# Routed experts visited two pairs at a time, and the shared expert's later row loads issued by GpSimd

## The chip, the cores and the metric

The kernel runs on one core of a Trainium2 chip. The metric is the device time of one execution in microseconds. A run's time is the median of several executions; the profile comes from one more execution that the hardware profiler recorded.

## The reference

All data is float32. A sequence of 64 steps with 128 rows of 512 values goes through a GRU, then a feed-forward layer with ternary weights, a causal convolution, and at last a mixture of experts. Only the last part is touched by the change. Cut to it:

```python
# x: [8192, 512]; 64 experts, 6 of them for each token, at most 64 tokens for an expert
scores = softmax(x @ gate_w.T)
topk_w, topk_i = top_k(scores, 6)
buf = zeros((64, 64 + 1, 512)).at[flat_i, slot].set(x[token_ids])
g = einsum('ech,ehi->eci', buf, w_gate)          # [64, 65, 352]
u = einsum('ech,ehi->eci', buf, w_up)
y = einsum('eci,eih->ech', silu(g) * u, w_down)
out_slots = y[flat_i, slot] * (flat_w * valid)[:, None]
routed = out_slots.reshape(T, 6, 512).sum(axis=1)
shared = silu(x @ sw_gate) * (x @ sw_up) @ sw_down   # [8192, 704] inside
result = x_in + routed + shared
```

So each of the 64 experts has 64 slots of gathered rows, a gate, an up and a down product; the shared expert sees every row.

## The kernel before, in words

The program runs in stages: the GRU with its input products and the ternary layer (to about 1400 us), the convolution (to about 1560 us), then the shared expert in 16 blocks of 4 time steps (512 rows). The router's work is laid between the products of blocks 0 to 8. From block 9 on (about 2022 us) the routed experts are laid there instead. Only blocks 9 to 15 matter here.

**The shared expert.** `shared(i)` computes block i with a fast scheme of seven half-size products (`winograd`, L695): each product is two matmuls (four records on TensorE) into one of four PSUM tiles `y`, `psx`, `psw`, `psz`. VectorE and ScalarE empty these tiles with sums (L726, L729, L731, L738, L741) and Silu. A block begins with four wide matmuls (L869) and ends with a down product (L806, L823) whose results are written over the block's rows `xr`. Each `yield` of `shared` is a slot, 44 a block; after each one the loop at the end of the kernel may call a piece of the routed experts. After a block `add_shared` (L971) issues four adding DMAs from GpSimd, from the block's rows into the output in DRAM. Then `load_xrows(i + 2)` (L1156) issues a load of 1 MB by SP into the same buffer, from the DRAM copy `xts`. There are two such buffers.

**The routed experts.** Two experts make a pair q: one expert's 64 slots use columns 0 to 63 of TensorE, the other's columns 64 to 127, so that the matmuls of both run side by side (records with 128\*64). These are the halved columns. For a pair there are four pieces of code:

- `inputs` (L1364 to L1371): VectorE copies the router's weights of the pair out of the gathered rows into `rw`; TensorE turns the rows (L1369) into `py`, and VectorE copies them to `xeT`.
- `gate_up` (L1382 to L1391): it first issues the gather of pair q + 2 (L1340, GpSimd, three `rows` buffers). 32 matmul calls give `pg` and `pu`; ScalarE's Silu and a product on VectorE with `rw` and `pu` make `a`.
- `turn` (L1397 to L1400): it first issues the loads of the gate and up weights of pair q + 2 by SP, into the buffers that pair q's matmuls have left; then TensorE turns `a` into `py`, and VectorE copies it to `aeT`.
- `down` (L1408 to L1419): the down product into `py`; the loads of the down weights of pair q + 2; ScalarE copies `py` to `ys` (L1417, two buffers); GpSimd scatters the two halves of `ys` into the output with two indirect, adding DMAs (L1419). Each of these waits until the one before it has landed, because both add into the same DRAM tensor.

The PSUM tiles `pg`, `pu`, `py` have one buffer each; the pool `ex` (`rw`, `xeT`, `a`, `aeT`, `ys`) has two. The weights of four experts, that is of two pairs, have room at a time.

**The order.** `experts()` yields 97 pieces: inputs, gate and up of pair 0, and then for each pair `turn`, the next pair's `inputs`, and one visit of the halved columns, that is `down` of pair q with `gate_up` of pair q + 1. The loop at the end of the kernel spreads them over 23/28 of the slots of blocks 9 to 15:

```python
while due < EPIECES and due * PIECES * SPREAD < slot * 4 * EPIECES:
    next(routed)
    due += 1
```

The text above gives the order in which the program is written. A scheduler then places the instructions on their engines, and each engine runs its own in the order in which they then stand. This moves gathers ahead by some pairs, for example. What is said of an order on an engine is read from the built program or the trace. For block 15 the output so far is loaded into a row buffer as `sums`, and the block's results are added there and stored by SP.

Of the kernel before, what the change touches and what calls it, by code (L numbers as in the profile page):

```python
# [42 lines left out]
def adaln_ffn_kernel(  # L43
# [22 lines left out]
    nc = tc.nc  # L66
# [32 lines left out]
    def load_rows(dst, src):  # L99

        return nc.sync.dma_start(out=dst, in_=src.rearrange("(k p) n -> p k n", p=P))
# [568 lines left out]
    NI = T // NB  # L670
# [303 lines left out]
    with (  # L974
# [10 lines left out]
        def turn(t):  # L985

            if t in (2, 3):
                ps = ps_y.tile([P, D], F32, name="y")
            else:
                ps = ps_t1.tile([P, D], F32, name="pst1")  # L990
            ps = ps.rearrange("p (k b) -> p k b", k=KD)
            for k in range(KD):
                last = nc.tensor.transpose(ps[:, k, :], hid(t)[:, k * P : (k + 1) * P], ident)
            return ps, last

        def route(its, turned={}):


            for i in its:
                for t in range(i * NB, i * NB + NB):  # L1000
                    ps = turned[t] if t in turned else turn(t)[0]
                    with behind(marks, t in turned):
                        copied = nc.vector.tensor_copy(
                            hid(t).rearrange("p (k b) -> p k b", k=KD), ps
                        )
                    if t == NB - 1:
                        marks.append(copied)
                    if t >= TH:
                        nc.sync.dma_start(out=xts[t - TH], in_=hid(t))
                    yield  # L1010
# [104 lines left out]
        for t in (NB, NB + 1):  # L1115
            second[t], last = turn(t)
# [36 lines left out]
    def load_xrows(i):  # L1153
        if i < NI:
            xrows[i] = xrp[i % 2].tile([P, NB, D], F32, name="xr")
            nc.sync.dma_start(  # L1156
                out=xrows[i], in_=xts[i * NB - TH : (i + 1) * NB - TH].rearrange("t p d -> p t d")
            )

    row_buffer("left")  # L1160
    load_xrows(NI // 2)
    esp = ctx.enter_context(tc.tile_pool(name="es", bufs=1, reuse_waits="tile"))
    wexs = []
# [15 lines left out]
    def load_gate_up(q):  # L1179

        if q < NE // 2:
            for e in (2 * q, 2 * q + 1):
                wg = wexs[e % 4].tile([P, KD, EI], F32, name="wg")
                load_rows(wg, w_gate[e])
                wu = wexs[e % 4].tile([P, KD, EI], F32, name="wu")
                load_rows(wu, w_up[e])
                weights[e] = [wg, wu]

    def load_down(q):
        if q < NE // 2:  # L1190
            for e in (2 * q, 2 * q + 1):
                wd = wexs[e % 4].tile([P, len(ech), D], F32, name="wd")
                load_rows(wd[:, :efull, :], w_down[e, : efull * P, :])
                nc.sync.dma_start(out=wd[:n_last, efull, :], in_=w_down[e, efull * P :, :])
                weights[e].append(wd)

    weights = {}
    for q in range(2):
        load_gate_up(q)
        load_down(q)  # L1200
    load_xrows(NI // 2 + 1)

    NPAIR = NE // 2
# [125 lines left out]

    add_shared(NI // 2)
    load_xrows(NI // 2 + 2)
    gat = ctx.enter_context(tc.tile_pool(name="gat", bufs=3, reuse_waits="tile"))
    ex = ctx.enter_context(tc.tile_pool(name="ex", bufs=2, reuse_waits="tile"))
    ps_e = ctx.enter_context(tc.tile_pool(name="ps_e", bufs=1, space=PSUM))

    def gather(q):
        rows = gat.tile([P, TW], F32, name="rows")
        nc.gpsimd.indirect_dma_start(  # L1340
            out=rows,
            out_offset=None,
            in_=tab,
            in_offset=bass.IndirectOffsetOnAxis(ap=idxp[:, q : q + 1], axis=0),
        )
        return rows
# [4 lines left out]
    class Pair:  # L1351
# [5 lines left out]
        def inputs(self):  # L1357
            q = self.q
            rows = gathered.pop(q)
            self.ws = [weights.pop(2 * q + j) for j in range(2)]  # L1360

            self.rw = ex.tile([P, 1], F32, name="rw")
            for j in range(2):
                nc.vector.tensor_copy(  # L1364
                    self.rw[halves[j]], rows[halves[j], D + 2 * q + j : D + 2 * q + j + 1]
                )
            ps = ps_e.tile([P, D], F32, name="py").rearrange("p (k b) -> p k b", k=KD)
            for k in range(KD):
                nc.tensor.transpose(ps[:, k, :], rows[:, k * P : (k + 1) * P], ident)  # L1369
            self.xeT = ex.tile([P, KD, P], F32, name="xeT")  # L1370
            nc.vector.tensor_copy(self.xeT, ps)  # L1371

        def gate_up(self):
            q = self.q
            if q + 2 < NPAIR:
                gathered[q + 2] = gather(q + 2)
            pg = ps_e.tile([P, EI], F32, name="pg")
            pu = ps_e.tile([P, EI], F32, name="pu")
            for which, acc in ((0, pg), (1, pu)):
                for k in range(KD):  # L1380
                    for j in range(2):
                        nc.tensor.matmul(  # L1382
                            acc[halves[j]],
                            self.xeT[:, k, halves[j]],
                            self.ws[j][which][:, k, :],
                            start=(k == 0),
                            stop=(k == KD - 1),
                        )
            self.a = a = ex.tile([P, EI], F32, name="a")
            nc.scalar.activation(a, pg, AF.Silu)  # L1390
            nc.vector.scalar_tensor_tensor(a, a, self.rw, pu, ALU.mult, ALU.mult)  # L1391

        def turn(self):
            load_gate_up(self.q + 2)
            ps = ps_e.tile([P, D], F32, name="py").rearrange("p (k b) -> p k b", k=KD)
            for c, (i0, n) in enumerate(ech):
                nc.tensor.transpose(ps[:n, c, :], self.a[:, i0 : i0 + n], ident)  # L1397
            self.aeT = aeT = ex.tile([P, len(ech), P], F32, name="aeT")
            nc.vector.tensor_copy(aeT[:, :efull, :], ps[:, :efull, :])
            nc.vector.tensor_copy(aeT[:n_last, efull, :], ps[:n_last, efull, :])  # L1400

        def down(self):

            q = self.q
            py = ps_e.tile([P, D], F32, name="py")
            for c, (i0, n) in enumerate(ech):
                for j in range(2):
                    nc.tensor.matmul(  # L1408
                        py[halves[j]],
                        self.aeT[:n, c, halves[j]],  # L1410
                        self.ws[j][2][:n, c, :],
                        start=(c == 0),
                        stop=(c == len(ech) - 1),
                    )
            load_down(q + 2)
            ys = ex.tile([P, D], F32, name="ys")
            nc.scalar.copy(ys, py)  # L1417
            for j in range(2):
                nc.gpsimd.indirect_dma_start(  # L1419
                    out=out,  # L1420
                    out_offset=bass.IndirectOffsetOnAxis(
                        ap=(idxp[:CAP] if j == 0 else idxo)[:, q : q + 1], axis=0
                    ),
                    in_=ys[halves[j]],
                    in_offset=None,
                    compute_op=ALU.add,
                )

    EPIECES = 3 * NPAIR + 1

    def experts():
        pairs = [Pair(q) for q in range(NPAIR)]
        pairs[0].inputs()
        yield
        pairs[0].gate_up()
        yield
        for q, pair in enumerate(pairs):
            pair.turn()  # L1440
            yield
            if q + 1 < NPAIR:
                pairs[q + 1].inputs()
                yield
            pair.down()
            if q + 1 < NPAIR:
                pairs[q + 1].gate_up()
            yield

    routed = experts()  # L1450
    SPREAD = 23
    slot = due = 0
    for i in range(NI // 2 + 1, NI):
# [8 lines left out]
        for _ in shared(i, sums):  # L1462
            slot += 1
            while due < EPIECES and due * PIECES * SPREAD < slot * 4 * EPIECES:
                next(routed)
# [53 lines left out]
```

## Time and profile before

| what | value |
|---|---|
| median of 3 runs | 2658.8 us (2657.62 to 2659.84) |
| the profiled execution | 2660.39 us, span 2658.7 us |
| TensorE (PE) busy | 2633.1 us, 11959 matmul records |
| VectorE (DVE), ScalarE (ACT), GpSimd (POOL) busy | 1411.4, 422.7, 457.4 us |
| mean granted TensorE clock | 0.999 |
| DMA from 2050 to 2550 us | share of the 16 engines 0.82 to 1.07 by stretches of 50 us, 242 to 344 GB/s |
| gate and up matmuls (L1382) | 1024 records, 459 ns median |
| down matmuls (L1408) | 384 records, 592 ns median |
| first and last record of the down matmuls | 2040.9 and 2579.5 us |
| gathers (L1340) | 32, 1046 ns issue, 6.1 us to landing |
| scatters (L1419) | 64, 1422 ns issue, 7.2 and 6.4 us to landing (first and second half) |
| row loads (L1156) by SP | 8 of 1 MB, 5.7 us to landing |

How to read it: a profile shows one execution. Times are in microseconds from the span's start unless they are marked ns. PE is TensorE's matmuls, PEld its weight loads, which overlap with them. Matmuls are pipelined, so a matmul's length is more than what it costs; the distance between two starts is the cost. A line number is that of the kernel before. `out<-in` names the tiles written and read, and the form after it gives rows\*columns of the array and partitions x elements. "to landing" counts from a DMA's issue to the end of its transfer.

### The profile page before, as it was taken

How to read it: one execution, taken by the hardware profiler on the slowest of the kernel's cores; microseconds unless marked ns; L12 is line 12 of the kernel's file. 1: busy time of each engine (PE TensorE's matmuls, PEld its weight loads, DVE VectorE, ACT ScalarE, POOL GpSimd, SP SyncE). 2: the span in 40 equal slices, each digit the busy share in tenths (PEclk: the TensorE clock that was granted, in tenths of full speed). 3: DMA queues.
4: the chain of work that ended last, by engine and by line, in shares of the span. 5: the costliest groups of instructions: out<-in, count | busy, mean ns of one | idle time of the engine just before them, and what ended most of it. 6: DMA issues, size and time to landing. Idle time of an engine off the chain costs nothing. (4 is left out here: it accounts for less than half of the span.)

```text
span 2658.7 us, 31099 instructions
## 1 busy us (share of the span) xinstructions
PE 2633.1 (99%) x11959; PEld 1817.7 (68%) x11959; DVE 1411.4 (53%) x3116; ACT 422.7 (16%) x779; POOL 457.4 (17%) x519
## 2 busy tenths in 40 slices
PE   8999999999999999999999999999999999999999
PEld 5666666666666666666668767788876666666667
DVE  6555555555555555555557755666564333434344
ACT  1111111111111111111110222222321111111111
POOL 2112111111112121111114100000001222222210
PEclk9999999999999999999999999999999999999999
DMA  5323232332322222322238921122356899998952
GB/s 194 69 56 62 54 67 56 63 61 54 60 47 52 44 52 44 76 44 52 44 63 285 331 43 27 38 64 64 79 153 172 290 309 287 294 327 269 295 176 48
DMA packets 475540, 323.33 MB, mean 122 GB/s; under 512 B 328960, under 2 KB 395136, under 8 KB 473216
## 3 DMA queue, kind: packets, MB, share of 16 engines
q1 hardware_dynamic: 446800, 248.18, 33.4%
q0 software_dynamic: 28592, 73.16, 11.4%
q8 instruction: 95, 1.56, 0.2%
q14 instruction: 53, 0.43, 0.0%
HBM read 235.01 MB, written 92.55 MB: 123 GB/s over the span
## 5 line engine op out<-in xcount | busy, mean ns | idle before, releaser
L502 PE MATMUL psgh<-whh,hT 128*128 128x512 f32 x1536 | 676.3, 596 | 0.7 <-ACT hT L399 0.7
L502 PEld LDWEIGHTS psgh<-whh,hT 128*128 128x128 f32 x1536 | 287.2, 190 | 351.3 <-issue 337.2
L338 PE MATMUL psx<-wih,xp 128*128 128x256 f32 x768 | 198.5, 381 | 6.4 <-DMA wih<-in_w_ih_dram 5.9
L220 POOL DMA_DIRECT2D xn<-in_x_dram x61 | 33.8, 555 | 840.8 <-DVE x L428 829.2
L338 PEld LDWEIGHTS psx<-wih,xp 128*128 128x128 f32 x768 | 143.7, 191 | 25.7 <-issue 5.9
L512 DVE TENSOR_TENSOR n<-psgh,bhn 128x512 f32<-128x512 f32 x64 | 44.2, 691 | 175.4 <-PE psgh L502 175.4
L1391 DVE SCALAR_TENSOR_TENSOR a<-a,rw,pu 128x352 f32<-128x352 f32 x32 | 18.6, 580 | 220.9 <-PE pu L1382 220.9
L399 ACT COPY hT<-psf 128x512 f32<-128x512 f32 x64 | 37.5, 585 | 584.0 <-PE psf L393 584.0
L509 DVE TENSOR_TENSOR r<-psgh,gi 128x512 f32<-128x512 f32 x64 | 44.2, 691 | 141.6 <-PE psgh L502 141.6
L971 POOL DMA_DIRECT2D out_dram<-hid x32 | 27.6, 1000 | 454.6 <-issue 335.9
L413 POOL TENSOR_TENSOR xn<-xn,fb 128x512 f32<-128x512 f32 x64 | 80.7, 1263 | 144.6 <-DMA xn<-in_x_dram 144.6
L338 PE MATMUL psz<-wih,xs 128*128 128x256 f32 x384 | 98.7, 379 | 1.8 <-DVE gi L361 1.8
L338 PE MATMUL psy<-t,xs 128*128 128x256 f32 x384 | 99.9, 383 | 0.2 <-DVE t L289 0.2
L338 PE MATMUL psw<-t,xp 128*128 128x256 f32 x384 | 98.8, 380 | 0.4 <-DVE u L359 0.4
L338 PE MATMUL psw<-wih,xp 128*128 128x256 f32 x384 | 98.7, 379 | 0.0
L338 PE MATMUL psz<-t,xs 128*128 128x256 f32 x384 | 98.7, 379 | 0.0
L417 PE MATMUL psf<-sgn,hhi 128*128 128x512 f32 x256 | 95.0, 493 | 0.3 <-DVE hlo L407 0.3
L1408 PE MATMUL py<-wd,aeT 128*64 128x512 f32 (+1 forms) x384 | 89.5, 601 | 0.0
L353 DVE TENSOR_TENSOR p<-psx,bi 128x512 f32<-128x512 f32 x96 | 66.3, 691 | 37.5 <-PE psx L338 37.2
L515 ACT ACTIVATE n<-n 128x512 f32<-128x512 f32 x64 | 40.3, 629 | 274.1 <-DVE n L514 274.1
L695 PE MATMUL psx<-xr,swg 128*128 128x256 f32 x320 | 83.3, 383 | 0.0
L695 PE MATMUL psx<-hid,swg 128*128 128x256 f32 x320 | 82.4, 380 | 0.0
(311 smaller groups left out, 4709.9 us busy)
## 6 DMA issues: line engine op xcount, KB each, us to landing
wg<-in_w_gate_dram SPq DMA_DIRECT2D x64, 704.0 KB, 10.4
wu<-in_w_up_dram SPq DMA_DIRECT2D x64, 704.0 KB, 11.3
wd<-in_w_down_dram SPq DMA_DIRECT2D x64, 512.0 KB, 7.9
x1c<-x SPq DMA_DIRECT2D x62, 256.0 KB, 5.2
out_dram<-x SPq DMA_DIRECT2D x62, 256.0 KB, 5.5
xn<-in_x_dram POOLq DMA_DIRECT2D x61, 256.0 KB, 4.1
xp<-in_xT_dram POOLq DMA_DIRECT2D x30, 512.0 KB, 5.3
xc<-x1c SPq DMA_DIRECT2D x28, 512.0 KB, 8.2
```

The costliest lines, as they stand in the source:

```text
L220: (nc.sync if t < 3 else nc.gpsimd).dma_start(out=xn, in_=x[:, t, :])
L338: i = nc.tensor.matmul(ps, self.ops[n][:, k, :], self.ws[n][:, k, :], start=(first and k == 0), stop=(k == HK - 1), skip_group_check=not f ...
L353: add(self.p1, both, b)
L399: nc.scalar.copy(hT, ps)
L413: nc.gpsimd.tensor_add(xn, xn, fb)
L417: nc.tensor.matmul(ps, piece[:, k, :], sgn[:, k, :], start=(i == 0 and k == 0), stop=(i == 1 and k == KD - 1),)
L502: nc.tensor.matmul(ps, hT[:, k, :], whh[c][:, k, :], start=(k == 0), stop=(k == KD - 1))
L509: nc.vector.tensor_add(r, ps_r, gis.pop((t, 0)))
L512: nc.vector.tensor_add(n, ps_n, bhn)
L515: nc.scalar.activation(n, n, AF.Tanh)
L695: i = nc.tensor.matmul(ps.rearrange("p (j b) -> p j b", b=P) if len(r.shape) == 3 else ps, lhs(k), r, start=(first and k == 0), stop=(k == ...
L1408: nc.tensor.matmul(py[halves[j]], self.aeT[:n, c, halves[j]], self.ws[j][2][:n, c, :], start=(c == 0), stop=(c == len(ech) - 1),)
```

## The change

Four things are changed.

1. The row loads of blocks 10 to 15 are issued by GpSimd and no longer by SP. Those of blocks 8 and 9 stay on SP.
2. `experts()` takes two pairs in a round: `turn` of both, `inputs` of the next two, and then one visit with `down` q, `gate_up` q + 2, `down` q + 1, `gate_up` q + 3. At the start the inputs of pairs 0 and 1 come first, and then both their `gate_up`.
3. The loads of the gate and up weights of pair q + 2 are issued in `gate_up`, behind the matmuls, and no longer in `turn`.
4. The pieces are 81 and no longer 97, which changes their spacing in slots. The weights are kept in a dictionary by expert and kind, since gate, up and down weights are now stored in another order.

```diff
     def load_xrows(i):
         if i < NI:
             xrows[i] = xrp[i % 2].tile([P, NB, D], F32, name="xr")
-            nc.sync.dma_start(
+
+            (nc.sync if i < NI // 2 + 2 else nc.gpsimd).dma_start(
                 out=xrows[i], in_=xts[i * NB - TH : (i + 1) * NB - TH].rearrange("t p d -> p t d")
             )
...
-                weights[e] = [wg, wu]
+                weights.setdefault(e, {}).update({0: wg, 1: wu})
...
-                weights[e].append(wd)
+                weights.setdefault(e, {})[2] = wd
...
-            self.ws = [weights.pop(2 * q + j) for j in range(2)]
+            self.ws = [weights[2 * q + j] for j in range(2)]
...
+            load_gate_up(q + 2)
             self.a = a = ex.tile([P, EI], F32, name="a")
...
         def turn(self):
-            load_gate_up(self.q + 2)
...
-    EPIECES = 3 * NPAIR + 1
+    EPIECES = 5 * NPAIR // 2 + 1

     def experts():
         pairs = [Pair(q) for q in range(NPAIR)]
-        pairs[0].inputs()
+        for pair in pairs[:2]:
+            pair.inputs()
+            yield
+        for pair in pairs[:2]:
+            pair.gate_up()
         yield
-        pairs[0].gate_up()
-        yield
-        for q, pair in enumerate(pairs):
-            pair.turn()
-            yield
-            if q + 1 < NPAIR:
-                pairs[q + 1].inputs()
+        for q in range(0, NPAIR, 2):
+            for pair in pairs[q : q + 2]:
+                pair.turn()
                 yield
-            pair.down()
-            if q + 1 < NPAIR:
-                pairs[q + 1].gate_up()
+            for pair in pairs[q + 2 : q + 4]:
+                pair.inputs()
+                yield
+            for pair in pairs[q : q + 2]:
+                pair.down()
+                if pair.q + 2 < NPAIR:
+                    pairs[pair.q + 2].gate_up()
             yield
```

## The prediction

> **What bounds the kernel now.** I read the busy times first, then the time by stretches, then TensorE's timeline in the stage that the change touches, then GpSimd's.
>
> ```profile
> PE 2633.1 (99%) x11959; PEld 1817.7 (68%) x11959; DVE 1411.4 (53%) x3116; ACT 422.7 (16%) x779; POOL 457.4 (17%) x519
> ```
>
> TensorE is busy 99% of the span. In the table by stretches (columns: span of the stretch; busy time of PE, PEld, DVE, ACT, POOL; clock; DMA share; GB/s) the routed experts, 2028 to 2580 us, look like this:
>
> ```profile
> 2150.00:2200.00 50.00, 50.00 (x276) 31.20 (x272) 18.40 (x47) 7.49 (x17) 13.03 (x10) 1.00 1.07 344
> 2200.00:2250.00 50.00, 50.00 (x257) 34.04 (x256) 20.34 (x51) 6.52 (x15) 13.22 (x12) 1.00 0.93 266
> ```
>
> No stretch from 2050 to 2600 us shows idle TensorE, the clock is full, and VectorE works 40% of the time. So a saving counts only if it shortens TensorE's own work there, and any new wait of TensorE is paid in full. But the DMA engines are as good as always busy too.
>
> One visit of the halved columns (64 of 128 columns: L1408, L1382), start and length in us:
>
> ```profile
> 2054.41 1.03 PE L695 MATMUL psz<-es,swu 128*128 128x256 f32 x4
> 2055.27 1.03 PE L695 MATMUL psx<-xr,swg 128*128 128x256 f32 x4
> 2056.23 2.80 PE L1408 MATMUL py<-wd,aeT 128*64 128x512 f32 x12
> 2058.86 2.54 PE L1382 MATMUL pg<-wg,xeT 128*64 128x352 f32 x16
> 2061.23 2.54 PE L1382 MATMUL pu<-wu,xeT 128*64 128x352 f32 x16
> 2063.69 1.13 PE L695 MATMUL psw<-xr,st 128*128 128x256 f32 x4
> 2064.66 1.03 PE L695 MATMUL psz<-es,st 128*128 128x256 f32 x4
> ```
>
> Read starts, not lengths. A product of the shared expert takes 0.86 from start to start (2054.41 to 2055.27), but 0.96 when a visit follows (2055.27 to 2056.23) and 0.97 when one came before (2063.69 to 2064.66). pg takes 2.37, and pu, with the way back behind it, 2.46. The first matmuls of a visit are longer too, as the spread of the down product (min/median/max ns) shows:
>
> ```profile
> L1408 PE MATMUL py<-wd,aeT x384: 590/592/643, 2040.9 to 2579.5; 128*64 128x512 f32 x128, 96*64 96x512 f32 x64
> ```
>
> So entering and leaving costs 0.10 + 0.05 + 0.09 + 0.11 = **0.35 us** a visit, beside 2.63 + 2.37 + 2.37 = 7.37 of work. From down to gate, both halved, nothing is added.
>
> GpSimd's queue (start, length, idle time before):
>
> ```profile
> 2125.91 3.63 POOL L971 DMA_DIRECT2D out_dram<-xr  x4 [5.49 <-issue]
> 2129.84 1.07 POOL L1340 DMA_INDIRECT rows<-tab,idxp  x1 [0.30 <-PE psx L695]
> 2136.67 1.47 POOL L1419 DMA_INDIRECT out_dram<-ys,idxp  x1 [5.75 <-ACT a L1390]
> 2144.72 1.41 POOL L1419 DMA_INDIRECT out_dram<-ys,idxo  x1 [6.58 <-DMA out_dram<-ys,idxp]
> ...
> 2196.65 1.42 POOL L1419 DMA_INDIRECT out_dram<-ys,idxp  x1 [4.33 <-DMA out_dram<-ys,idxo]
> ```
>
> GpSimd is busy 17%, yet its queue is nearly full: each scatter waits until the one before it has landed, since both add into the output. From 2136.67 to 2196.65 stand 8 scatters: 7.50 each, 15.0 for a pair, where a pair of experts comes every 15.34 (2040.9, 2056.23, 2071.6). By the DMA table's medians (7.2 and 6.4 to landing, 0.27 to the next issue) a scatter takes 7.07. This queue is the second bound.
>
> **The change, part by part.**
>
> *Visits.* Before: pair 0's gate, 31 visits of down and gate, a last down: 33. As built, the changed order has one double gate, 15 double visits, and the last two downs apart, since a shared product stands between them: 18. 15 fewer x 0.35 = **-5.2 us**, all of it on the path. Matmuls, transposes and evictions stay as many.
>
> *Within a double visit* (down q, gate q+2, down q+1, gate q+3, 14.7 us) the single PSUM buffers are met again. py comes back 4.74 after down q ends; its copy takes 0.585. pg comes back 5.0 after it ends, its Silu takes 0.463. pu comes back 5.0 later, its product takes 0.58. Covered, so 0; without the cover one such eviction, 0.6 x 16.
>
> *Weights.* The loads of gate and up move from the next pair's transposes to right behind the matmuls that free the buffer; SP issues as many. They come in bursts of two pairs. The slowest up load lands 15.6 after its issue now; the second pair's burst stands 7.4 after the first's instead of 15.3, so at most 8 more queue ahead of it: 23.6. It is issued at 14.7 of a visit and needed at 30.3 + 12.4 = 42.7, so 28 are there. 0; if the cover goes, each us late is paid once a visit, up to 16.
>
> *Row loads on GpSimd.* Six loads leave SP. GpSimd's order at a block's end becomes four adds (L971), the load, which must wait until the adds have landed because it overwrites their rows, and then the gathers. No 1 MB load from GpSimd is in the trace: its issue lies between 0.72 (512 KB, L214) and, twice that, 1.44; 256 KB takes 0.555, so 0.16 for each further 256 KB gives 1.05, which I take. SP is relieved: at 2136.02 it issued such a load just after the adds had landed, and the down weights behind it went at 2136.47, though their matmuls had ended at 2133.1. Nobody waited for them, so that gains 0.
>
> The Trainium skill, in "DMA: Bandwidth & Descriptors", section "Issuing engines are not separate DMA queues", says that the issuing engine makes no difference to a transfer, as all share 16 DMA engines, and only the sequencer's issue time is saved, usually little. By that rule this part would be worth 0 and the sum -5.2, 2653.6. The rows above say that an in-order queue costs more than its issue times, through what waits in it.
>
> *The new wait.* As built, VectorE's order after a double visit is: a, rw, a, rw, then the shared expert's sums. rw (L1364) needs the gathered rows of a pair used a whole visit later, and if they are late, the sums behind it are late, and TensorE's PSUM buffers with them. Times from a visit's first down, V: its first scatter goes at 2.63 + 0.24 + 0.585 + 0.27 = 3.7. The gather behind the block's end lands after four scatters, the adds (10.6 until the last has landed, from 2125.91), the load (1.05 + 0.3) and its own median 6.1: V + 3.7 + 4s + 12 + 6.1. With s = 7.07 that is V + 50.1, with 7.50 V + 51.8. rw wants it at the next visit's end, 14.7 + 0.2 + 0.58 = 15.5 after its start. Double visits stand 2 x 15.34 - 0.35 = 30.33 apart, more where a block ends, by the products that the built order puts between them: 42.1 after pair 2 (57.6, spare), 36.6 after pair 8 (52.1, just enough), 32.0 after pair 14 (two products fewer, -1.73, and the four wide matmuls of L869, +3.4): 47.5, **2.6 to 4.3 late**. In the fourth and fifth block the gathers stand ahead of the load. Behind that visit TensorE has 4 products and a transpose, 3.8, that need no VectorE; VectorE needs 0.3 for rw and 2 x 0.42 for two sums first. So of the lateness 2.0 are covered: +0.6 to +2.3. I take **+1.7**, nearer the dense row.
>
> *What is carried on.* The scatters of pair 16 then start 12.6 late, and in dense stretches 30.33 - 4 x 7.5 = 0.3 a visit is won back. ys has two buffers: the copy of pair 19 waits until the last scatter of pair 17 has landed, at V16 + 46.3 instead of 40.5. ScalarE's next Silu and VectorE's a come 2.0 late, which the cover above just holds. Bounds: 0, and 3 if it happens there and once more after the next block; I take **+1.0**.
>
> *Cadence.* EPIECES falls from 97 to 81 and pieces come every 3.12 products instead of 2.61: as many pairs per product. 0.
>
> Sum: -5.2 + 1.7 + 1.0 = -2.5. The profiled execution took 2660.4 (span 2658.7 and 1.7 around it), 1.6 above the runs' median of 2658.8; the profile would come to 2657.9, the median to **2656.3 us**.
>
> **Rivals.**
> 1. *Nothing waits.* The rows land in time because scatters take 7.07 or less: 2653.6. For it: VectorE works only 40%, and scatters after 2560 take 4. Against: the 7.50 of the dense stretch.
> 2. *Slower: the scatters set the pace.* In place: GpSimd's queue from 2060 to 2570. 62 scatters and 5 block ends (10.6 + 1.35 + two gathers of 1.3, 14.5) need 62s + 73; there are 510, and some 12 that the two ys buffers let it lag: it decides from s = 7.24 on. At 7.07 it needs 511, at 7.50 538: 16 too much, less the 5.2: +11, though the lighter stretches (6.6 at 2044 and 2112) halve that: 2664 to 2669. For it: gathers that used to hide in scatters' waits now stand behind the load. Against: the queue caught up several times before (ys done just ahead of the scatter at 2304.84).
> 3. *Weights late* by the bursts: each visit 1 us, 2670. Against: the 4.4 to spare.
>
> **How the numbers follow.** About 0.2% (5.3 us) is what a measurement of this kernel can tell from no change. Forecast 0.53, all within it. Rival 1 0.20: at 5.2 it lies on the border, 0.12 beyond and 0.08 within. Rival 2 0.22, all slower. Rival 3 0.05: 0.03 slower, 0.02 within. So faster 0.12, within 0.63, slower 0.25. The range goes from rival 1 less a run's scatter of 0.8 to the near end of rival 2 and a little more: 2652.8 to 2665.
>
> **What the changed profile would show.** The entry and exit of 0.35 only 18 times; no idle between halved products. Idle TensorE of some 2 us about 2350, put down to VectorE sums (L726, L729), with rw before them waiting for DMA rows. The lag from ys to its first scatter near 12 for pair 16. The forecast is wrong if scatters average over 7.3 there (rival 2), or if no matmul of the shared expert waits (rival 1).

## The result and the profile after

The changed kernel takes 2664.63 us (median of 11; 2662.7 to 2668.47) and the kernel before, on the same chip, 2658.18 (11; 2657.51 to 2660.34): ratio 1.0021, 95% interval 1.0013 to 1.0028. It is slower by 6.45 us; the forecast was 2.5 faster. The profiled execution took 2664.47, span 2662.8.

I read the busy times and the stretches first, as before (columns as there).

```profile
PE 2630.0 (99%) x11959; PEld 1821.9 (68%) x11959; DVE 1410.8 (53%) x3116; ACT 422.9 (16%) x779; POOL 461.9 (17%) x525
```

```profile
2150.00:2200.00 50.00, 50.00 (x271) 33.79 (x271) 20.41 (x51) 7.12 (x17) 12.52 (x10) 1.00 0.95 302
2200.00:2250.00 50.00, 50.00 (x270) 30.69 (x267) 15.96 (x40) 6.54 (x15) 12.14 (x11) 1.00 0.99 291
...
2350.00:2400.00 50.00, 40.90 (x207) 28.18 (x206) 17.46 (x48) 5.62 (x13) 14.78 (x12) 0.90 0.96 309
```

TensorE has less work than before (2630.0 against 2633.1). Every stretch of 50 us from 2050 to 2600 is full but one, and that one also has a clock of 0.90. TensorE's timeline there (start, length, and in brackets the idle time before and who ended it):

```profile
2351.53 1.03 PE L695 MATMUL psz<-es,swu 128*128 128x256 f32 x4
2352.40 0.49 PE L1398 MATMUL py<-ident,a 128*128 128x128 f32 x3
2352.72 1.03 PE L695 MATMUL psx<-xr,swg 128*128 128x256 f32 x4
2362.85 2.08 PE L695 MATMUL psw<-xr,st 128*128 128x256 f32 x4 [9.10 <-DVE u L729]
2364.72 1.91 PE L695 MATMUL psz<-es,st 128*128 128x256 f32 x4
```

One gap of 9.10 us, ended by a VectorE sum. The four matmuls after it take 1.87 from start to start, where those at 2351.53 took 0.87: half the clock. Stretches cut to the gap show it in the clock column (the last but two):

```profile
2353.00:2362.80 9.80, 0.75 (x4) 0.33 (x2) 1.14 (x5) 0.00 (x0) 3.50 (x3) 0.73 1.06 369
2362.80:2367.80 5.00, 4.95 (x12) 3.96 (x13) 2.46 (x7) 0.80 (x2) 1.41 (x1) 0.50 1.06 329
2367.80:2380.00 12.20, 12.20 (x65) 8.94 (x65) 5.63 (x13) 1.63 (x5) 4.02 (x4) 1.00 0.73 215
```

Ten records start 0.427 apart and not 0.216, and the first is 0.37 late: 2.5 us more. VectorE's timeline says why the sum was late:

```profile
2349.92 0.58 DVE L1393 SCALAR_TENSOR_TENSOR a<-a,rw,pu 128x352 f32<-128x352 f32 x1 [6.39 <-PE pu L1383]
2361.51 0.31 DVE L1365 COPY rw<-rows 64x1 f32<-64x1 f32 x2 [11.01 <-DMA rows<-tab,idxp]
2361.85 0.42 DVE L726 TENSOR_TENSOR u<-u,y 128x256 f32<-128x256 f32 x1
2362.37 0.42 DVE L729 TENSOR_TENSOR u<-psw,u 128x256 f32<-128x256 f32 x1
```

Two copies of one column each, `rw`, which nobody needs before the next visit, wait 11.01 us for a gather, and both sums stand behind them. GpSimd's queue shows what the gather stood behind:

```profile
2306.68 1.46 POOL L1420 DMA_INDIRECT out_dram<-ys,idxp  x1 [6.44 <-ACT ys L1418]
2314.26 1.42 POOL L1420 DMA_INDIRECT out_dram<-ys,idxo  x1 [6.12 <-DMA out_dram<-ys,idxp]
2322.68 1.40 POOL L1420 DMA_INDIRECT out_dram<-ys,idxp  x1 [7.00 <-ACT u L724]
2330.39 1.40 POOL L1420 DMA_INDIRECT out_dram<-ys,idxo  x1 [6.30 <-DMA out_dram<-ys,idxp]
2337.21 3.63 POOL L971 DMA_DIRECT2D out_dram<-xr  x4 [5.43 <-DMA out_dram<-ys,idxo]
2351.33 0.79 POOL L1157 DMA_DIRECT2D xr<-xts  x1 [10.48 <-DMA out_dram<-xr]
2353.00 1.05 POOL L1341 DMA_INDIRECT rows<-tab,idxp  x1 [0.89 <-PE py L1398]
```

Four scatters, four additions, the load of rows, which waits 10.48 for the additions, and only then the gather. The chain of waits gives its landing:

```profile
2353.00 8.41 DMA rows<-tab,idxp
```

To set kernels side by side I use a **stretch**: from the first product of L869 in block 9 to the last product of L823. Before it is 2022.34 to 2653.80, 631.46; after 2020.05 to 2658.00, 637.95, 6.5 more. The sum closes: 15 entries and exits saved, -5.1 (measured alone in the third experiment group below), the gap +9.1, the half clock +2.5. What lies ahead of block 9 varies by some us (its start lies between 2016.3 and 2023.8 in the eleven traces), so that medians say less than the stretch. The stretch is read from one execution, but the three kernels with one pair in a visit agree in it to 0.01.

### The profile page after: what moved, and what is told of

Its sections match the earlier page's. It is cut to its first block, busy times and chain, and to the rows that moved or that the text cites. A ratio compares the mean times of both kernels' runs of the same rounds, so it can differ in the third digit from the quotient of the medians.

```text
span 2662.8 us, 31119 instructions
## 1 busy us (share of the span) xinstructions
PE 2630.0 (99%) x11959; PEld 1821.9 (68%) x11959; DVE 1410.8 (53%) x3116; ACT 422.9 (16%) x779; POOL 461.9 (17%) x525
```

## The experiments

Medians are of 11 executions (e6: 6).

| kernel | median | before, measured alongside | ratio and 95% interval | stretch |
|---|---|---|---|---|
| the changed kernel | 2664.63 | 2658.18 | 1.0021 (1.0013 to 1.0028) | 637.95 |
| e1 pairs, loads on SP | 2659.05 | 2659.14 | 1.0001 (0.9992 to 1.0010) | 629.29 |
| e2 before, loads on GpSimd | 2658.55 | 2659.14 | 1.0000 (0.9991 to 1.0009) | 631.45 |
| e3 rw behind xeT | 2658.15 | 2659.14 | 0.9998 (0.9989 to 1.0007) | 632.70 |
| e4 load behind a gather | 2661.30 | 2659.14 | 1.0010 (1.0001 to 1.0019) | 631.84 |
| e6 e3 and four ys buffers | 2651.88 | 2659.83 | 0.9970 (0.9958 to 0.9982) | 626.36 |
| e7 e1, load behind weights | 2656.03 | 2659.83 | 0.9987 (0.9978 to 0.9996) | 629.00 |
| e8 four ys buffers only | 2665.02 | 2659.83 | 1.0018 (1.0009 to 1.0027) | 638.01 |
| e9 before, e6's two mends | 2656.82 | 2658.66 | 0.9989 (0.9980 to 0.9998) | 631.45 |
| e10 e6, loads on SP | 2656.97 | 2658.66 | 0.9993 (0.9984 to 1.0002) | 632.70 |

### First group: which part makes the gap

Theory 1 is the reading above: pairs, load and rw together make the gap. Theory 2: the load on GpSimd costs by itself. Theory 3: the pairing costs by itself, through the scatters and gathers that it brings close together.

**e1** undoes the move of the loads.

```diff
-            (nc.sync if i < NI // 2 + 2 else nc.gpsimd).dma_start(
+            nc.sync.dma_start(
```

> Two pairs in one visit, all loads of rows back on SyncE's queue. Theory 1 (the order of the two queues: VectorE's rw copy stands a visit ahead, and the gather it needs stands on GpSimd behind the load of rows, which waits until the additions have landed): without the load the gather of about 2353.0 is issued right behind the additions, about 2342, and lands at 8.4 us after that, about 2350, when VectorE comes to rw (2350.5). No wait, no clock drop, only the 15 saved entries and exits: 2653 (2652 to 2655), no gap over 1 us at L695 about 2352. Theory 2 (the load on GpSimd costs by itself, wherever rw stands): 2653 too. Theory 3 (the pairing itself costs: four scatters in a row and two gathers hold GpSimd's queue): 2663 to 2665, with the gap still there.

**e2** makes that move alone, in the kernel before.

```diff
-            nc.sync.dma_start(
+            (nc.sync if i < NI // 2 + 2 else nc.gpsimd).dma_start(
```

> The kernel before, with nothing but the later loads of rows moved to GpSimd's queue; one pair in a visit. Theory 1: here the gather issued behind the additions (2323.2 in the trace of before, put off to about 2334 by the load's wait) is wanted by rw two visits later, about 2363, so nothing is late: 2658 to 2660. Theory 2: the load's wait of about 10 us for the additions is paid here as well: 2664 to 2670. Theory 3: 2658.

**e3** moves only the two small copies on VectorE.

```diff
-            self.rw = ex.tile([P, 1], F32, name="rw")
-            for j in range(2):
-                nc.vector.tensor_copy(
-                    self.rw[halves[j]], rows[halves[j], D + 2 * q + j : D + 2 * q + j + 1]
-                )
...
-            nc.vector.tensor_copy(self.xeT, ps)
+            turned = nc.vector.tensor_copy(self.xeT, ps)
+            self.rw = ex.tile([P, 1], F32, name="rw")
+            with tc.issue_after(turned.ins):
+                for j in range(2):
+                    nc.vector.tensor_copy(
+                        self.rw[halves[j]], rows[halves[j], D + 2 * q + j : D + 2 * q + j + 1]
+                    )
```

> The changed kernel with the loads of rows left on GpSimd; only the two small copies of rw are put behind the copy of xeT on VectorE (same operations, same GpSimd order), so that the sums of the shared expert no longer stand behind them. Theory 1: the gather still lands at about 2361 but VectorE has no business with it until the transposes of the next visit, so the 9.1 us gap and the 4.6 us of half clock both go: 2653 (2652 to 2655). Theory 2 (the load holds up something other than rw, scatters or the transposes): 2659 to 2665. Theory 3: 2663 to 2665.

**e4** lets one gather go ahead of the load.

```diff
         def gather(q):
...
+        with tc.issue_after(got.ins):
+            while owed and q % 2:
+                load_xrows(owed.pop())
...
-            load_xrows(i + 2)
+            owed.append(i + 2)
```

> The changed kernel with the load of rows still on GpSimd but issued behind the next gather instead of ahead of it; the next-but-one gather stands behind it. rw is left ahead, as in the changed kernel. Theory 1: the gather goes out right behind the additions, about 2342, and lands about 2350, at most 0.5 late, which the 1.9 us that TensorE has in hand cover: 2653 (2652 to 2655). Theory 2: the load and its wait are still on GpSimd, so most of the loss stays: 2659 to 2665. Theory 3: 2663 to 2665.

The 9.1 us gap is gone in e1, e3 and e4, and e2 is as long as before to 0.01 us. So neither part makes the gap alone: it takes the pairs, the load ahead of the gather, and rw ahead of the sums, and taking away any one of the three removes it. Theory 2 falls (e2, e3); theory 3, that the pairs keep the same gap whatever is moved, falls too. But the expected 2653 came in none of the three. Each has a new gap some 30 us later, at the next double visit. In e3 it is ScalarE that is late:

```profile
2384.35 0.55 PE L1399 MATMUL py<-ident,a 128*128 128x128 f32 x3 [2.48 <-ACT ys L1419]
2385.67 1.13 PE L695 MATMUL psz<-es,st 128*128 128x256 f32 x4 [0.77 <-DVE aT L741]
```

```profile
2383.71 0.58 ACT L1419 COPY ys<-py 128x512 f32<-128x512 f32 x1 [13.78 <-DMA out_dram<-ys,idxo]
```

The copy out of `py` waits 13.78 us for a scatter that still reads one of the two `ys` buffers, and the transposes wait for `py`. Two gaps of 2.48 and 0.77 follow, a third of 0.25, and then eight records at half clock. e4 has the same waits (13.5 on ScalarE; gaps of 2.19 and 1.23). Its median is 2.2 above before, though its stretch is only 0.4 longer; the profiled execution was the shortest of eleven, and what the others waited for isn't shown.

In e1 another queue is late, SyncE's (SPq, the DMA queue's own rows):

```profile
2328.77 2.42 SPq L101 DMA_DIRECT2D wu<-in_w_up_dram  x1
2348.91 0.37 SPq L1157 DMA_DIRECT2D xr<-xts  x1
2349.37 0.92 SPq L101 DMA_DIRECT2D wd<-in_w_down_dram  x1
```

```profile
2382.02 2.28 PE L1383 MATMUL pg<-wg,xeT 128*64 128x352 f32 x13 [1.80 <-DMA wg<-in_w_gate_dram]
```

The load waits for the additions, and the weights behind it wait with it: the first leaves 9.4 after the first addition (2339.93), where in the changed kernel it left 0.5 after it (2337.75 and 2337.21). So a second theory, 1b: **waits stand one behind the other**, and the first hides the next, because while TensorE stands still the scatters and the weights catch up.

### Second group: is the second wait the two ys buffers, or the weights' place?

**e6** adds to e3, and **e8** to the changed kernel, four buffers for `ys`; **e7** is e1 with the load issued behind the next gate and up weights.

```diff
+    ysp = ctx.enter_context(tc.tile_pool(name="ysp", bufs=4, reuse_waits="tile"))
...
-            ys = ex.tile([P, D], F32, name="ys")
+            ys = ysp.tile([P, D], F32, name="ys")
```

> e3 (rw behind xeT, loads of rows on GpSimd) with four buffers for ys in place of two. Theory 1b (two waits stand one behind the other: the rw wait, and once it is gone the wait of ScalarE's copy ys for the scatters that still read the two ys buffers, 13.8 us at about 2383 in e3's trace, of which 2.5 and 0.8 us and 11 half-clock products reach TensorE): with four buffers both are gone, only the saved entries and exits are left: 2653 (652 to 655 after the 2000), that is 5 us below before in the same call, and no gap over 1 us between 2030 and 2600. Theory 3 (the pairing costs somewhere whatever is freed): a third gap appears, in the gathers or the additions, and the time stays at 2657 to 2660.

> The changed kernel with four buffers for ys and nothing else; rw stays ahead, loads of rows stay on GpSimd. Theory 1b: the first wait (rw, gather behind additions and load) does not ask about ys: the 9.1 us gap and the 4.6 us of half clock stay, 2663 to 2665, 5 to 7 above before. A rival (two ys buffers, by delaying the scatters, are what made the gather late): the gather comes earlier and the time falls to 2655 to 2659.

```diff
-                load_rows(wu, w_up[e])
+                last = load_rows(wu, w_up[e])
...
+            with tc.issue_after(last.ins):
+                while owed and q % 2:
+                    load_xrows(owed.pop())
...
-            load_xrows(i + 2)
+            owed.append(i + 2)
```

> e1 (all loads of rows on SyncE's queue) with each load issued behind the weights of the following visit instead of ahead of them; rw ahead and two ys buffers as in the changed kernel. Theory 1b: in e1 the load waited on SyncE's queue for the additions (issued 2348.9) and the weights stood behind it, which is the 1.8 us gap for wg about 2382 and about 1 us of spread waits behind it; here they go first, so that the 3 us come back and the saved entries stay: 2653 to 2655, 4 to 5 us below before. Theory 4 (the gap for wg in e1 comes from the number of transfers in flight, not from the order): the gap stays and so does e1's time, as before within 1.

e6 stands 7.95 below before (4.8 to 11.2 by the interval), the fastest kernel here, and no third gap appears. The stretch where the changed kernel lost its time:

```profile
2350.00:2400.00 50.00, 50.00 (x268) 36.50 (x267) 23.95 (x63) 6.37 (x15) 13.22 (x11) 1.00 1.06 345
```

e8 keeps the first gap (9.87, with the half clock behind it): more ys buffers don't help while rw stands ahead. e7's gap for wg is gone and its median is 3.8 below before, but a gap of 2.56 is left at 2488, of the kind seen in e3: ScalarE's copy of `ys` waits 10.33 for a scatter, then `a`, rw and the sums behind them are late.

```profile
2485.14 0.58 ACT L1423 COPY ys<-py 128x512 f32<-128x512 f32 x1 [10.33 <-DMA out_dram<-ys,idxo]
```

```profile
2488.44 1.13 PE L695 MATMUL psz<-es,swu 128*128 128x256 f32 x4 [2.56 <-DVE aT L731]
```

### Third group: what each part is worth once the waits are eased

**e9** is the kernel before with e6's two edits (shown above); **e10** is e6 with e1's edit.

> The kernel before with the two mends of e6 alone (rw behind the copy of xeT, four buffers for ys): one pair in a visit, all loads of rows on SyncE's queue. Theory 1b: in the trace of before the rw copies wait once, about 1999, for the first gathers (1.48 and 0.89 us, and TensorE idles 0.57, 0.53 and 0.25 there); that goes, some 1.8 us, and nothing else of before waited on either: 1 to 2.5 below before, 2657 to 2658.5 where before stands at 2659.5; from the first product of L869 on as long as before, 631.4 within 0.2. So e6's 8 us under before would be about 2 of the mends and 5 to 6 of the pairing. Rival: the mends by themselves are worth most of e6's gain (5 to 8 below before), and the pairing is worth little.

> e6 with the loads of rows back on SyncE's queue, ahead of the weights of the next visit, as before the change: pairs in one visit, rw behind xeT, four buffers for ys. Theory 1b: the load waits there for the additions and holds the weights behind it, as in e1; the gap for wg about 2382 (1.8 us, 3 with the waits spread behind it) is back, the other gaps stay gone: 2 to 4 above e6, that is 4 to 6 below before; from the first product of L869 629 to 630 against e6's 626.4. So the move of the loads is worth about 3 where nothing else waits. Rival (step 4 of the prediction: relieving SyncE is worth nothing, e1's gap was of that run): as e6 within 1.

e9 stands 1.84 below its before (0.5 to 5.3 by the interval), and its stretch is unchanged. So the gain lies ahead of it, where the prediction had not looked: VectorE's timeline of the kernel *before*.

```profile
1999.42 0.31 DVE L1364 COPY rw<-rows 64x1 f32<-64x1 f32 x2 [1.48 <-DMA rows<-tab,idxp]
1999.77 0.42 DVE L729 TENSOR_TENSOR u<-psw,u 128x256 f32<-128x256 f32 x1
2001.08 0.31 DVE L1364 COPY rw<-rows 64x1 f32<-64x1 f32 x2 [0.89 <-DMA rows<-tab,idxp]
```

The wait that cost 9.1 us after the change was there before it, at 1.48 and 0.89, when the first gathers land. TensorE stood still for 0.57, 0.53 and 0.25 behind it, 1.35 in all; in e6, e9 and e10 none of this is left.

From e9 to e6 the stretch falls from 631.45 to 626.36: **pairs and moved loads together are worth 5.1**. Of e6's 7.95, then, 5.1 are theirs and 1.35 the early waits; the rest, 1.5, is inside the interval's width and isn't assigned. From e6 to e10 it rises to 632.70: with the loads on SP the wait for wg is back, larger than in e1, with some 6 us of half clock behind it, of which half is lost. That is 2.8 and 3.0 of the 6.3, where I expected about 3.

```profile
2375.04 4.37 PE L1385 MATMUL pg<-wg,xeT 128*64 128x352 f32 x13 [2.76 <-DMA wg<-in_w_gate_dram]
```

```profile
2371.90:2375.00 3.10, 0.39 (x2) 0.00 (x0) 0.00 (x0) 0.46 (x1) 1.45 (x1) 0.86 1.03 391
2375.00:2381.00 6.00, 5.96 (x22) 2.47 (x24) 0.00 (x0) 0.46 (x1) 0.85 (x1) 0.50 1.07 319
```

So taking the loads from their place ahead of the weights is a needed half of the pairing, not an ornament: pairs with the loads left there are no faster than one pair in a visit (stretch 632.70 against 631.45, medians 2656.97 and 2656.82), although they have 5.1 less to do. GpSimd's queue is one place to take them to; behind the weights on SP is another: e7's stretch less its ys gap is 629.00 - 2.56 = 626.44, that of e6.

## Why the prediction was wrong

- *Visits, -5.2:* right. 18 entries and exits, and the stretch falls by 5.1 where nothing waits (e9 to e6).
- *PSUM buffers within a double visit, 0:* right, no gap within one in the changed kernel or in e6.
- *Weights, 0:* right with the loads on GpSimd, where no matmul waits for them. It rested on the loads having left SP, which the step did not say (e1, e10).
- *Row loads:* the issue took 0.79, within the bounds and under the 1.05 taken. "Nobody waited for them, so that gains 0" holds for the old order (e2: 0.0) and fails for the new one, where the move is worth 6.3 (e10 against e6).
- *The new wait, +1.7:* **this is the step that failed, by its size.** Place, queue and order were as told: the visit of pair 16, rw behind the gather, the idle time put down to the sum of L729; the cover was 11.0 - 9.1 = 1.9 where 2.0 was said. But the rows were 11.0 late and not 2.6 to 4.3. From the 4.3 that s = 7.50 gave: four scatters took 30.5 and not 30.0 (+0.5); from the first addition to the load 14.1 and not 10.6 (+3.5; the row from which the 10.6 comes gives 10.1 to SP's load, at 2136.02, and 10.6 to the weights behind it); from the load to the gather 1.7 and not 1.35 (+0.3); the gather landed after 8.4 and not 6.1 (+2.3). That makes 10.9.
- The two large terms have one origin. The 10.6 and the 6.1 came from rows of the old order, where SP's load waited for the additions and **held back the weights meanwhile**. The change takes away this hold. Before:

```profile
2318.74 3.61 POOL L971 DMA_DIRECT2D out_dram<-xr  x4 [5.55 <-DVE xr L843]
2328.11 0.37 SPq L1156 DMA_DIRECT2D xr<-xts  x1
2328.57 0.46 SPq L101 DMA_DIRECT2D wd<-in_w_down_dram  x1
```

  After, beside the additions of 2337.21 and the load of 2351.33:

```profile
2337.75 0.37 SPq L101 DMA_DIRECT2D wd<-in_w_down_dram  x1
```

  From the first addition to the load's issue it is 9.4 before, 9.0 in e1 and 9.3 in e10, each with SP standing still; it is 14.1 in the changed kernel and 13.5 in e3, where the weights started 0.5 and 1.2 after the first addition. Which queue issues the load isn't it: in e2, with the load on GpSimd, it is 9.3 where the first weights leave only 8.1 after the first addition (2325.71), and at the two next such block ends, where they leave 4.6 and 4.0 after it (from 2426.00 and 2516.12), 11.3 and 9.8. The changed kernel itself has 9.7 a block earlier (from 2227.70), where they leave 6.4 after it. The gather goes the same way: 5.4 to landing before (2323.21) and 5.8 in e1, with the weights held, 9.9 in e2 (2327.92) beside them. So, of the block ends at which the four additions are issued in one go, 13 and more stand only where the weights leave almost with them; that the shared transfers cause it is a reading, as no run changed these alone.
- *What is carried on, +1.0:* nothing of it in the changed kernel, since the 9 us gap let the scatters catch up. The mechanism was right: once the gap is gone (e3) it comes at the predicted place, ScalarE's copy of ys, and costs more than the bound of 3: the stretch is 6.3 longer than e6's.
- *Cadence, 0:* right (e6).
- *Left out:* the half clock after a gap, 2.5 us, which with the gap's 9.1 less the 5.1 saved makes the 6.5. Against the forecast that is 7.4 from the new wait (9.1 for 1.7) and 2.5 from the clock, less the 1.0 that wasn't carried on.

Rival 2 named nearly the measured time, but for another reason, which is luck. Scatters took 7.63 on the way to the gap, above its 7.24 and above the 7.3 that the prediction gave as its sign. But the scatters' pace didn't make the gap: it was the gather behind the load that ended it, TensorE has no other gap between 2030 and 2600, and e6 has 7.55 on the same way and none. Only with rw out of the way does the scatters' lag reach TensorE, through the two ys buffers (e3).

The rule "Issuing engines are not separate DMA queues" of the Trainium skill's page "DMA: Bandwidth & Descriptors", which the prediction weighed, would again give 0 for the move of the loads. In the old order e2 agrees (0.0); in the new one e10 against e6 measures 6.3 for it, through what stands behind the load in an in-order queue.

## What to carry to other kernels

When a change lets a transfer start earlier, take the durations of its neighbours from rows in which such transfers run beside each other, not from rows in which a wait kept them apart. A small copy that waits for a DMA belongs on its engine's queue where its result is needed, not a visit ahead: everything behind it waits as well. And when a gap is taken away, look at once for the wait that it covered: here three queues (VectorE's rw, ScalarE's ys, SyncE's weights) had to be eased together before all 5 us of saved work could be seen.

## What the runs showed of the hardware

A gap can cost more than its length. After 9.1 us of idle TensorE the granted clock was 0.50 for about 5 us of work; after 2.76 us (e10) it was 0.50 for about 6, and after 2.48 and 0.77 with three transposes between them (e3) eight records were at half rate; after 2.56 (e7) and 1.80 (e1) it stayed at 1.00.

The Trainium skill, in "TensorE: Matmul & The Clock Gate", section "Part 1: The HAM clock gate", says that the clock is halved after an idle window of about 3.4 us and restored after about as long a busy one, and that the window runs freely. The 9.1 us gap agrees: the mean clock of 0.73 over 9.8 us means half clock for the last 5.3 of them, so that it fell some 4 us into the gap, and it came back about 5 us after work did. In e10 a gap of 2.76, shorter than the window, was enough, so that 3.4 us is no safe bound below which a gap costs only itself.
